# Attention scores from float32r halves, with heads interleaved by on-chip transfers

## The chip, the core and the metric

The kernel runs on one core of a Trainium2 chip. Its engines work side by side, each with its own queue of instructions: TensorE (PE, with weight loads as PEld), VectorE (DVE), ScalarE (ACT), GpSimd (POOL) and SyncE (SP), which here only issues DMAs. The metric is the device time of one execution in microseconds (us); three executions are given by their median and ends.

## The reference, cut to what matters

The program is a block of four sublayers on x of 8 batches x 512 tokens x 256 channels. Only the first, an attention with selected queries, is touched:

```python
q, k, v = split_heads(xn @ Wq + bq), split_heads(xn @ Wk + bk), split_heads(xn @ Wv + bv)
scores   = einsum('bhqd,bhkd->bhqk', q, k) / sqrt(16)          # 16 heads of 16 channels
sparsity = scores.max(-1) - scores.mean(-1)
top      = top_k(sparsity, 307)                                # of 512 queries
out[top] = softmax(scores[top]) @ v                            # the others stay zero
x = x + out @ Wo + bo
```

After it come a routed feed-forward layer, a gated linear attention with a SwiGLU layer, and the feed-forward layer again.

## The kernel before, in words

**What a score is for.** Every score is computed twice. `max_one` (line 531) makes a 128 x 512 tile with queries on the partitions and reduces it to row maxima on DVE (L541). `exp_one` (line 545) makes the transposed tile, keys on the partitions, and ACT takes its exponential (L553). `weigh` (L558) multiplies the exponentials by the values; a column of ones among the values gives the denominators. Keys are centred over the tokens (`xcT`), so that the mean of the scores needs no computing, and exponentials are of score minus maximum.

**Layout.** A chunk `m` is half of the channels, 8 heads, in four strips of 32 partitions. A strip holds an even head (e = 0) in its first 16 rows and an odd one (e = 1) in the last 16. Scores need one head at a time, so each head is kept in a copy in which the other head's rows are zero: `qs[e]` is made with a scale `own` that is one or zero by row, and `ks[e]` with a scale `kept`. One row of the other head's 16 does work: in `ks[e]` it is set to one, and in `qs[e]` it takes the negated row maximum, so that the product over 32 rows gives score minus maximum at once.

**Maxima to queries.** `place_maxima` (line 494) turns the maxima of a batch's chunk by a TensorE transpose (`mxT`, L501), negates them on ACT (L506), and issues transfers of 4 rows x 128 on SP (L510): 8 into `qs` and 8 into `neg`, the tile from which `top_queries` later chooses queries on DVE. These are the placements.

**Steps.** The loop at line 664 goes over steps n, 16 per batch (two chunks, two parities e, four tiles). Step n computes maxima for batch n // 16 and exponentials for the step 16 earlier (LAG), and weighs the exponentials of one step before. A step has two halves; each issues four score products, two for exponentials and two for maxima, one in each row strip. After the first half comes the weighing, after the second one piece of a `front` (line 392): the transposition, projection and evacuation of a later batch, cut in 14 pieces by `yield`. Fronts 0 and 1 run early; the front of batch b >= 2 has its pieces in the steps from LEAD + 16 (b - 2), and none in the two steps of EMPTY, which weigh in two half widths instead. From step 112 on, every fourth step does one more step of maxima. Maxima end at step 123; the exponentials go on to step 143, while DVE makes the choice of queries.

**Evacuation of a front.** Per chunk, q is read from PSUM twice (L449 on DVE; in the early fronts L444 on ACT) and k twice on ACT (L461).

**PSUM.** Score tiles come from two rings of banks, three for exponentials (`bank`) and four (`bank_m`) for maxima, fronts and `mxT`; one bank accumulates the weighing.

**Order.** Each engine takes its instructions in the order of the program. That holds for SP's transfers too: one that waits holds up those behind it.

Of the kernel before, what the change touches and what calls it, by code (L numbers as in the profile page):

```python
# [10 lines left out]
F32 = mybir.dt.float32  # L11
U8 = mybir.dt.uint8
I32 = mybir.dt.int32
# [5 lines left out]
P = 128  # L19
# [20 lines left out]
def block_kernel(ctx: ExitStack, tc: tile.TileContext, t: dict, out: bass.AP):  # L40
# [57 lines left out]

    share = ctx.enter_context(tc.tile_pool(name="share", bufs=1))
# [3 lines left out]
    with ExitStack() as outer:  # L103
# [28 lines left out]
        rden = a_out.tile([P, L], F32, name="rden")  # L132
        work = a_out.tile([P, L + 8], F32, name="work")
        m8 = a_out.tile([P, 8], F32, name="m8")

# [42 lines left out]
        with ExitStack() as inner:  # L178
# [15 lines left out]
            def load_heads(name, src, eng):  # L194

                wp = a2.tile([P, NC2, L], F32, tag="k1", name=name + "_pad", bufs=3)
                eng.dma_start(out=wp, in_=src.rearrange("(c p) m -> p c m", p=P))
                w = a1.tile([P, NC2, D], F32, name=name)
                nc.gpsimd.tensor_copy(
                    w.rearrange("p c (h d) -> p (c h) d", d=DH),  # L200
                    wp.rearrange("p c (h q) -> p (c h) q", q=32)[:, :, 0:DH],
                )
                return w

            def load_head_column(name, src, eng):
                w = a1.tile([P, NC2], F32, name=name)
                for r in range(2):
                    eng.dma_start(
                        out=w[64 * r : 64 * r + 64, :],
                        in_=src.rearrange("(j q) g -> j q g", q=32)[:, 0:DH, r::2],  # L210
                    )
                return w
# [14 lines left out]
            marks = a1.tile([P, 3, 2], F32, name="marks")  # L227
            own, one, kept = (marks[:, i, :] for i in range(3))
            nc.vector.tensor_reduce(own[:, 0:1], head_of, AX.X, ALU.add)
            nc.vector.tensor_scalar(own[:, 1:2], own[:, 0:1], -1.0, 1.0, ALU.mult, ALU.add)  # L230
            for e in range(2):
                nc.vector.tensor_reduce(
                    one[:, e : e + 1], ident[:, DH * (1 - e) :: 32], AX.X, ALU.add
                )
            nc.vector.tensor_scalar(kept, one, -1.0, 1.0, ALU.mult, ALU.add)
            bq_own = a1.tile([P, 2, NC2], F32, name="bq_own")
            for e in range(2):
                nc.vector.tensor_scalar(bq_own[:, e, :], bq, own[:, e : e + 1], None, ALU.mult)

            bk_kept = a1.tile([P, 2, NC2], F32, name="bk_kept")  # L240
            nc.gpsimd.tensor_tensor(bk, bk, bk, ALU.subtract)
            for e in range(2):
                nc.vector.tensor_scalar(
                    bk_kept[:, e, :], bk, kept[:, e : e + 1], one[:, e : e + 1],
                    ALU.mult, ALU.add,
                )
# [4 lines left out]
                a1.tile([P, 4 * H // 2, 2, 32], F32, tag=f"va{i}", name=f"va{i}")  # L251
# [3 lines left out]
            def clear_values(i, late=None):  # L255
                va = vas[i]
                if late is not None:
                    nc.gpsimd.tensor_copy(va[0:1, 0, 0, 0:1], late)
                nc.gpsimd.memset(va, 0.0)
                nc.gpsimd.memset(va[:, :, 0, DH : DH + 1], 1.0)  # L260
                nc.gpsimd.memset(va[:, :, 1, 0:1], 1.0)

            clear_values(0)
            for i in range(2):
                nc.gpsimd.memset(den[i], 1.0)

# [85 lines left out]
            )  # L352
            for _ in batch_stats([0]):
                pass
# [26 lines left out]

            fronts = {}
# [9 lines left out]
            def front(b, pick, alone):  # L392
# [3 lines left out]
                xnT = a2.tile([P, NC2, L], F32, tag="xnT", name=f"xnT{b}")  # L396
# [4 lines left out]
                for c in range(NC2):  # L401
# [17 lines left out]
                qs = [  # L419
                    a2.tile([P, NC2, L], F32, tag=f"q{e}", name=f"q{e}_{b}", bufs=3)  # L420
                    for e in range(2)
                ]
                ks = [
                    a2.tile([P, NC2, L], F32, tag=f"k{e}", name=f"k{e}_{b}", bufs=3)
                    for e in range(2)
                ]
                va = vas[b % 3]
                fronts[b] = (qs, ks, va, xcT)
# [7 lines left out]
                for m in range(NC2):  # L436
                    ps = pick(f"q_ps{b}")
                    for c in range(NC2):
                        project(ps, wq, xnT, m, c)
                        if c == 0:  # L440
                            yield
                    for e in range(2):
                        if alone and (b + m > 0 or e == 0):
                            nc.scalar.activation(  # L444
                                qs[e][:, m, :], ps, AF.Identity,
                                bias=bq_own[:, e, m : m + 1], scale=own[:, e : e + 1],
                            )
                        else:
                            nc.vector.tensor_scalar(  # L449
                                qs[e][:, m, :], ps, bq[:, m : m + 1], own[:, e : e + 1],  # L450
                                ALU.add, ALU.mult,
                            )
                    yield

                    ps = pick(f"k_ps{b}")
                    for c in range(NC2):
                        project(ps, wk, xcT, m, c)
                        if c == 0:
                            yield
                    for e in range(2):  # L460
                        nc.scalar.activation(  # L461
                            ks[e][:, m, :], ps, AF.Identity,
                            bias=bk_kept[:, e, m : m + 1], scale=kept[:, e : e + 1],
                        )
                    yield
                for kp in range(2):
# [11 lines left out]
                    for e in range(2):  # L478
                        home = va[
                            :, 16 * kp : 16 * kp + 16, e, DH * e : DH * e + DH  # L480
# [12 lines left out]

            def place_maxima(b, m, es, tiles=range(4)):
# [10 lines left out]
                negT = a2.tile([32, P], F32, tag="negT", name=f"negT{b}")  # L505
                nc.scalar.mul(negT[0:rows, :], pt[0:rows, 0:P], -1.0)  # L506

                def place(target, r):
                    for i, k in enumerate(tiles):
                        nc.sync.dma_start(  # L510
                            out=target[:, bass.ts(k, P)],
                            in_=negT[r + 4 * i : r + 4 * i + 4, :],
                        )

                def to_queries():
                    for i, e in enumerate(es):
                        place(fronts[b][0][e][DH * (1 - e) :: 32, m, :], n * i)

                def to_choice():
                    for i, e in enumerate(es):  # L520
                        r = row_of(b, m, e)
                        place(neg[r : r + 4, :], n * i)
# [8 lines left out]
            def max_one(b, m, e, k, j, pick):  # L531


                qs, ks = fronts[b][0:2]
# [3 lines left out]
                nc.tensor.matmul(  # L538
                    s, qs[e][rows, m, bass.ts(k, P)], ks[e][rows, m, :], start=True, stop=True
                )  # L540
                nc.vector.tensor_reduce(  # L541
                    mx[:, b % 4, m, e, r : r + 1], s, AX.X, ALU.max
                )

            def exp_one(b, m, e, kt, j, pick):
                qs, ks = fronts[b][0:2]
                rows = bass.ts(j, 32)
                s = pick(f"s2_{b}")
                nc.tensor.matmul(  # L549
                    s, ks[e][rows, m, bass.ts(kt, P)], qs[e][rows, m, :], start=True, stop=True  # L550
                )
                ex = a2.tile([P, L], F32, tag="e", name=f"e{b}", bufs=10)
                nc.scalar.activation(ex, s, AF.Exp, scale=1.0 / DH**0.5)  # L553
                return ex

            def weigh(av, m, e, kt, es, va, queries):
                for j in range(4):
                    nc.tensor.matmul(  # L558
                        av[32 * j : 32 * j + 32, queries],
                        va[:, 8 * kt + 4 * m + j, e, :],  # L560
# [4 lines left out]
            def take(b, m, e, av):  # L565

                st = a2.tile([P, L], F32, tag=f"st{e}", name=f"st{e}_{b}")
# [36 lines left out]
            LEAD = 14  # L604
            EMPTY = (13, 14)
# [22 lines left out]
            def finish(item, part=None):  # L628
# [10 lines left out]
                weigh(av, m, e, kt, es, fronts[b][2], queries)  # L639
# [24 lines left out]
            for n in range(len(steps) + LAG + 1):  # L664
# [4 lines left out]
                empty = batch + 2 >= NB or i in EMPTY  # L669
                halves = LAG < n <= len(steps) and empty and (n - LAG - 1) % 4 > 0  # L670
                if ahead is None:
                    if here is not None:
                        for i in range(4):
                            es[i] = exp_one(*here, i, bank if i % 2 else bank_m)
                    for part in (0, 1) if halves else (None,):
                        finish(behind, part)
                elif here is None:
                    for i in range(4):
                        max_one(*ahead, i, bank if i % 2 else bank_m)
                    place_full(n)  # L680
                else:

                    for half in range(2):
                        for i in range(4):
                            if i % 2 == half:
                                es[i] = exp_one(*here, i, bank)
                            else:
                                max_one(*ahead, i, bank_m)
# [9 lines left out]
                if ahead is not None:  # L698
                    all_maxima(ahead)
                    if n >= 112 and n % 4 == 0 and coming < len(steps):  # L700
                        ahead = steps[coming]
                        for i in range(4):
                            max_one(*ahead, i, bank_m)
                        all_maxima(ahead)

                if n < LEAD:
# [17 lines left out]
                    while done < 22 * (n + 1) // LEAD:  # L724
                        next(pieces, None)
                        done += 1
                else:
                    if n >= LAG:
                        next(later, None)
                    if (n - LEAD) % 16 == 12 and batch + 3 < NB:  # L730
                        norm(batch + 3)
                        add_bias(batch + 3)
                    if (n - LEAD) % 16 == 0:
                        pieces = (
                            front(batch + 2, bank_m, False) if batch + 2 < NB else iter(())
                        )
# [682 lines left out]
```

## Time and profile before

| | us |
|---|---|
| median of 3 executions (lowest, highest) | 1606.35 (1604.23, 1610.29) |
| the profiled execution | 1611.02 |
| its span, first to last instruction | 1609.3 |
| first score product | 15.43 |
| first product for an exponential (step 16) | 61.0 |
| step 112, by its extra maxima | 465 |
| last product for a maximum ends | 515 |
| last exponential ends | 563 |
| L541 on DVE: 512 reductions, mean | 328.1, 0.683 |
| L553 on ACT: 512 exponentials, mean | 276.0, 0.597 |
| L538 on PE: 1024 records of max products, busy | 294.6 |
| L549 on PE: 1024 records of exp products, busy | 291.9 |
| L558 on PE: 1240 records of weighings, busy | 142.6 |

The granted TensorE clock is 0.995 of full speed. A fp32 product shows as two records, each with a weight load. Records of products in different row strips overlap, so a group's busy time is the union of its records, not their sum. The execution's time is 1.7 us over its span.

### The profile page before, as it was taken

What the parts mean: (1) busy time and instruction counts of PE and PEld (TensorE: products, weight loads), DVE (VectorE), ACT (ScalarE), POOL (GpSimd) and SP (SyncE); (2) the same over time, 40 slices, a digit from 0 to 9 for tenths busy, and PEclk for the clock granted to TensorE, in tenths of its full rate; (3) what the DMA queues carried; (4) which work ended last, traced back from release to release, by engine and by line L of the source; (5) the groups of instructions that cost most, each with busy time, mean ns of one, the idle gap of its engine ahead of it and who ended that gap; (6) DMA issues with size and microseconds to landing.
All of it is one profiled execution on the core that took longest, in us unless ns stands there. A gap on an engine that the chain in (4) does not pass through costs nothing.

```text
span 1609.3 us, 19898 instructions
## 1 busy us (share of the span) xinstructions
PE 1575.9 (98%) x7444; PEld 811.8 (50%) x7444; DVE 956.4 (59%) x1982; ACT 682.3 (42%) x1249; POOL 390.2 (24%) x470
## 2 busy tenths in 40 slices
PE   7999999999999999999999999999999999999999
PEld 3333323323233276655564567546545655756666
DVE  7888767677676984538744565456275533354332
ACT  5556656666566833442255125432531442121110
POOL 4423112021000151115433333234253320000000
PEclk9999999999999999999999999999999999999999
DMA  4100000000000051100000001000000010011100
GB/s 122 31 3 2 3 3 3 2 2 3 3 3 3 2 171 28 27 14 13 1 1 0 1 1 27 1 0 1 0 1 1 0 27 0 21 34 40 40 27 26
DMA packets 24968, 27.62 MB, mean 17 GB/s; under 512 B 6888, under 2 KB 21416, under 8 KB 24872
## 3 DMA queue, kind: packets, MB, share of 16 engines
q1 hardware_dynamic: 24056, 25.31, 5.5%
q8 instruction: 58, 0.95, 0.2%
q10 hardware_dynamic: 816, 1.05, 0.2%
q14 instruction: 38, 0.31, 0.1%
HBM read 21.24 MB, written 4.33 MB: 16 GB/s over the span
## 4 chain that ended last, share of the span: by engine, by line
PE 79%; DVE 11%; ACT 4%; POOL 3%; issue 2%; DMA 1%; SPq 0%; POOLq 0%; ACTq 0%; DVEq 0%
PE y_ps L1016 16%; PE h_ps L1042 10%; PE s L538 9%; PE s L549 9%; PE av L558 8%; PE swi_ps L1069 7%; PE proj_ps L1155 7%; DVE pr L1188 2%; DVE pr L1178 2%; PE q_ps L431 2%; POOL o L1205 2%; PE v_ps L470 2%; PE k_ps L431 2%; PE gla_y L1280 2%; DVE w L1180 2%
## 5 line engine op out<-in xcount | busy, mean ns | idle before, releaser
L541 DVE TENSOR_REDUCE mx<-s 128x1 f32<-128x512 f32 x512 | 328.1, 683 | 119.1 <-PE s L549 62.4
L553 ACT ACTIVATE e<-s 128x512 f32<-128x512 f32 x512 | 276.0, 597 | 180.2 <-PE s L549 104.6
L538 PE MATMUL s<-k,q 32*128 32x512 f32 x1024 | 294.6, 639 | 1.4 <-ACT k L461 0.9
L549 PE MATMUL s<-q,k 32*128 32x512 f32 x1024 | 291.9, 639 | 0.0
L1016 PE MATMUL y_ps<-w,h 128*128 128x256 f32 x1024 | 234.8, 384 | 7.4 <-DVE h L1051 6.8
L1042 PE MATMUL h_ps<-xnT,w 128*128 128x512 f32 x512 | 228.1, 594 | 0.0
L1016 PEld LDWEIGHTS y_ps<-w,h 128*128 128x128 f32 x1024 | 193.9, 192 | 45.3 <-issue 10.2
L1042 PEld LDWEIGHTS h_ps<-xnT,w 128*128 128x128 f32 x512 | 94.7, 190 | 106.3 <-issue 104.3
L558 PE MATMUL av<-e,va 128*32 128x512 f32 (+1 forms) x1240 | 142.6, 530 | 1.4 <-ACT st L568 1.4
L1051 DVE TENSOR_TENSOR h<-h,mk 128x512 f32<-128x512 f32 x128 | 95.7, 762 | 79.5 <-ACT h L1050 61.4
L1050 ACT ACTIVATE h<-h_ps,b 128x512 f32<-128x512 f32 x96 | 65.3, 685 | 177.2 <-PE h_ps L1042 177.2
L538 PEld LDWEIGHTS s<-k,q 32*128 32x128 f32 x1024 | 91.4, 183 | 89.6 <-DVE mx L541 50.5
L549 PEld LDWEIGHTS s<-q,k 32*128 32x128 f32 x1024 | 89.6, 183 | 74.7 <-ACT e L553 52.6
L1027 DVE TENSOR_TENSOR xres<-xres,y_ps 128x512 f32<-128x512 f32 x47 | 32.2, 685 | 155.6 <-PE y_ps L1016 118.4
L1069 PE MATMUL swi_ps<-zT,w_up 128*128 128x512 f32 x256 | 122.4, 598 | 0.3 <-DVE h L1078 0.3
L1069 PE MATMUL swi_ps<-zT,w_gate 128*128 128x512 f32 x256 | 122.3, 596 | 0.0
L1016 PE MATMUL y_ps<-w_down,h 128*128 128x256 f32 x512 | 117.7, 380 | 0.8 <-DVE h L1078 0.8
L1155 PE MATMUL proj_ps<-q_w,rT 128*128 128x512 f32 x256 | 115.4, 594 | 1.0 <-DVE gate L1161 0.9
L1016 PEld LDWEIGHTS y_ps<-w_down,h 128*128 128x128 f32 x512 | 95.1, 190 | 19.8 <-issue 7.2
L1075 ACT ACTIVATE h<-swi_ps 128x512 f32<-128x512 f32 x64 | 38.2, 596 | 143.5 <-PE swi_ps L1069 143.4
L1205 POOL TENSOR_TENSOR o<-o,pr 128x512 f32<-128x512 f32 (+2 forms) x56 | 82.2, 1469 | 59.0 <-DVE pr L1188 57.4
L924 POOL TENSOR_TENSOR xres<-xres,b 128x512 f32<-128x512 f32 x32 | 40.0, 1271 | 206.3 <-ACT row L863 183.8
(219 smaller groups left out, 1742.1 us busy)
## 6 DMA issues: line engine op xcount, KB each, us to landing
mk<-md SPq DMA_DIRECT2D x32, 256.0 KB
out<-xres SPq DMA_DIRECT2D x15, 256.0 KB
xres<-in_L_attn_a_x SPq DMA_DIRECT2D x7, 512.0 KB
q<-negT SPq DMA_DIRECT2D x128, 2.0 KB
neg<-negT SPq DMA_DIRECT2D x128, 2.0 KB
w<-in_f_w1T SPq DMA_DIRECT2D x1, 1024.0 KB
w<-in_f_w2T SPq DMA_DIRECT2D x1, 1024.0 KB
w_gate<-in_b_w_gateT SPq DMA_DIRECT2D x1, 1024.0 KB
```

Of the source, the lines that this page charges most:

```text
L538: nc.tensor.matmul(s, qs[e][rows, m, bass.ts(k, P)], ks[e][rows, m, :], start=True, stop=True)
L541: nc.vector.tensor_reduce(mx[:, b % 4, m, e, r : r + 1], s, AX.X, ALU.max)
L549: nc.tensor.matmul(s, ks[e][rows, m, bass.ts(kt, P)], qs[e][rows, m, :], start=True, stop=True)
L553: nc.scalar.activation(ex, s, AF.Exp, scale=1.0 / DH**0.5)
L558: nc.tensor.matmul(av[32 * j : 32 * j + 32, queries], va[:, 8 * kt + 4 * m + j, e, :], es[j][:, queries], start=(kt == 0), stop=(kt == 3 a ...
L1016: nc.tensor.matmul(y[0][:, bass.ts(i, D)], h[f][:, bass.ts(2 * u + i, P)], w[:, f, :], start=(f == 0), stop=(f == NF - 1),)
L1042: nc.tensor.matmul(ps, w1[:, c, bass.ts(f, P)], xT[g][:, c, :], start=(c == 0), stop=(c == NC2 - 1),)
L1050: nc.scalar.activation(hf, ps, AF.Relu, bias=b1[:, f : f + 1])
L1051: nc.vector.tensor_tensor(hf, hf, mk[g][:, f, :], ALU.mult)
L1069: nc.tensor.matmul(ps, w[:, c, bass.ts(f, P)], zT[g][:, c, :], start=(c == 0), stop=(c == NC2 - 1),)
L1155: nc.tensor.matmul(ps, rT[b // G4][:, c, bass.ts(b % G4, P)], q_w[:, c, m], start=(c == 0), stop=(c == NC2 - 1),)
L1205: nc.gpsimd.tensor_tensor(dst, dst, src, ALU.add)
```

## The change: what it does

- **Halves.** q, k and the negated maxima are each split in two tiles of type float32r: `hi`, the rounded value, written by ACT from PSUM, and `lo`, value minus `hi`, written by DVE (`scalar_tensor_tensor`); for the maxima `lo` is written by POOL, in the last batch by DVE.
- **Layout.** The weights' columns are permuted as they are loaded, so that a chunk's rows alternate between an even and an odd head's channels. From `half` tiles, transfers of 64 rows x 512 on SP (`move`) lay out, per chunk, `qh` (q's hi twice, in alternate rows), `ql` (q's lo twice) and `km` (k's hi and lo in alternate rows), each with one plane for each parity e. So all 32 rows of a strip hold one head. Per chunk that is 8 moves for q and 4 for k.
- **Scores.** A maximum's score is two products, `qh` with `km` and `ql` with `km`, summed in PSUM. An exponential's is three: the same two, and one over four rows with `tops`, the halves of the negated maxima of both parities, against `takes`, ones and zeros that choose a parity. `together` issues the four tiles' first products, then their second, then the exponentials' third. With fp32 each score was one product.
- **Placements.** Per chunk 16 transfers into `tops` instead of 8 into `qs`, and 8 into `neg` as before.
- **Values.** One column of ones, between the parities, serves both.
- **Order.** Fronts of batches 2 to 7 begin 7 steps later (LEAD 21 instead of 14) and run values and heads in turn; EMPTY is (14, 15). The early phase keeps its 14 steps (FIRST).
- **Room.** `qh`, `ql`, `km` have four buffers per chunk, `half` four, `tops` three tiles; `xnT` has one buffer, `st` is shared by both parities, `rden` is `neg`.

```diff
             def load_heads(name, src, eng):
-                nc.gpsimd.tensor_copy(
-                    w.rearrange("p c (h d) -> p (c h) d", d=DH),
-                    wp.rearrange("p c (h q) -> p (c h) q", q=32)[:, :, 0:DH],
-                )
+                for e in range(2):
+                    nc.gpsimd.tensor_copy(
+                        w.rearrange("p c (g d e) -> p (c g) d e", d=DH, e=2)[:, :, :, e],
+                        wp.rearrange("p c (g e q) -> p (c g) e q", e=2, q=32)[:, :, e, 0:DH],
+                    )
...
             def load_head_column(name, src, eng):
                 for r in range(2):
-                    eng.dma_start(
-                        out=w[64 * r : 64 * r + 64, :],
-                        in_=src.rearrange("(j q) g -> j q g", q=32)[:, 0:DH, r::2],
-                    )
+                    for e in range(2):
+                        eng.dma_start(
+                            out=w[64 * r + e : 64 * r + 64 : 2, :],
+                            in_=src.rearrange("(j q) g -> j q g", q=32)[e::2, 0:DH, r::2],
+                        )
...
+            def move(dst, src):
+
+                nc.sync.dma_start(out=dst.bitcast(I32), in_=src.bitcast(I32))
+
...
+                def halves(ps, bias):
+
+                    hi, lo = (
+                        a2.tile([P, L], F32, tag="half", name=f"half{b}", bufs=4)
+                        for i in range(2)
+                    )
+                    nc.scalar.activation(hi.bitcast(HALF), ps, AF.Identity, bias=bias)
+                    nc.vector.scalar_tensor_tensor(
+                        lo.bitcast(HALF), ps, bias, hi, ALU.add, ALU.subtract
+                    )
+                    return hi, lo
+
+                def heads_of_chunk(m):
+
+                    qh, ql, km = (
+                        a2.tile([P, 2, L], F32, tag=tag, name=f"{tag}{b}", bufs=4)
+                        for tag in ("qh", "ql", "km")
+                    )
+                    pairs[m] = qh, ql, km
...
-                    for e in range(2):
-                        if alone and (b + m > 0 or e == 0):
-                            nc.scalar.activation(
-                                qs[e][:, m, :], ps, AF.Identity,
-                                bias=bq_own[:, e, m : m + 1], scale=own[:, e : e + 1],
-                            )
-                        else:
-                            nc.vector.tensor_scalar(
-                                qs[e][:, m, :], ps, bq[:, m : m + 1], own[:, e : e + 1],
-                                ALU.add, ALU.mult,
-                            )
+                    for to, half in zip((qh, ql), halves(ps, bq[:, m : m + 1])):
+                        for e in range(2):
+                            for x in range(2):
+                                move(to[x::2, e, :], half[e::2, :])
...
-                    for e in range(2):
-                        nc.scalar.activation(
-                            ks[e][:, m, :], ps, AF.Identity,
-                            bias=bk_kept[:, e, m : m + 1], scale=kept[:, e : e + 1],
-                        )
+                    for x, half in enumerate(halves(ps, bk[:, m : m + 1])):
+                        for e in range(2):
+                            move(km[x::2, e, :], half[e::2, :])
...
                 nc.scalar.mul(negT[0:rows, :], pt[0:rows, 0:P], -1.0)
+                nc.scalar.mul(hi[0:rows, :].bitcast(HALF), pt[0:rows, 0:P], -1.0)
+                eng = nc.vector if b == NB - 1 else nc.gpsimd
+                eng.tensor_tensor(
+                    lo[0:rows, :].bitcast(HALF), negT[0:rows, :], hi[0:rows, :], ALU.subtract
+                )
...
                 def to_queries():
                     for i, e in enumerate(es):
-                        place(fronts[b][0][e][DH * (1 - e) :: 32, m, :], n * i)
+                        for x, half in enumerate((hi, lo)):
+                            place(tops[(2 * b + m) % 3][2 * e + x :: 32, :], half, n * i)
...
             def max_one(b, m, e, k, j, pick):
-                nc.tensor.matmul(
-                    s, qs[e][rows, m, bass.ts(k, P)], ks[e][rows, m, :], start=True, stop=True
-                )
+                def product(i):
+                    nc.tensor.matmul(
+                        s, (qh, ql)[i].bitcast(HALF)[rows, e, bass.ts(k, P)],
+                        km.bitcast(HALF)[rows, e, :], start=(i == 0), stop=(i == 1),
+                    )
...
             def exp_one(b, m, e, kt, j, pick):
-                nc.tensor.matmul(
-                    s, ks[e][rows, m, bass.ts(kt, P)], qs[e][rows, m, :], start=True, stop=True
-                )
+                def product(i):
+                    if i < 2:
+                        keys = km[rows, e, bass.ts(kt, P)]
+                        queries = (qh, ql)[i][rows, e, :]
+                    else:
+                        four = slice(32 * j, 32 * j + 4)
+                        keys = takes[four, e, :]
+                        queries = tops[(2 * b + m) % 3][four, :]
+                    nc.tensor.matmul(
+                        s, keys.bitcast(HALF), queries.bitcast(HALF),
+                        start=(i == 0), stop=(i == 2),
+                    )
...
+            def together(items):
+
+                for i in range(3):
+                    for products, _ in items:
+                        if i < len(products):
+                            products[i]()
+                return [end() for _, end in items]
...
                     for half in range(2):
-                        for i in range(4):
-                            if i % 2 == half:
-                                es[i] = exp_one(*here, i, bank)
-                            else:
-                                max_one(*ahead, i, bank_m)
+                        made = together([
+                            exp_one(*here, i, bank) if i % 2 == half
+                            else max_one(*ahead, i, bank_m)
+                            for i in range(4)
+                        ])
+                        es[half::2] = made[half::2]
...
-            LEAD = 14
-            EMPTY = (13, 14)
+            FIRST = 14
+            LEAD = 21
+            EMPTY = (14, 15)
```

## Prediction

> **What bounds the kernel now.** First the page: which engine is full where.
>
> ```profile
> span 1609.3 us, 19898 instructions
> ...
> PE   7999999999999999999999999999999999999999
> PEld 3333323323233276655564567546545655756666
> DVE  7888767677676984538744565456275533354332
> ACT  5556656666566833442255125432531442121110
> ```
>
> One slice is 40.2 us. The change touches only the attention, slices 1 to 14 (to 564 us); the rest is taken as unchanged. PE stands at 9 throughout, but ends of matmuls are modelled, so I asked the chain of waits from 129 to 465 us:
>
> ```profile
> by line: PE s L538 27.8%; PE s L549 26.7%; PE av L558 24.6%; PE v_ps L470 6.3%; PE q_ps L431 6.3%; PE k_ps L431 6.3%; PE xnT_ps L404 1.6%; PE mxT_ps L501 0.6%
> ```
>
> It is PE alone, over half of it score products. The windows give the other engines' slack in one batch of 16 steps (332 to 399 us; columns: length, then busy time of PE, PEld, DVE, ACT, POOL):
>
> ```profile
> 332.00:399.00 67.00, 67.00 (x450) 20.61 (x444) 47.56 (x78) 41.20 (x79) 10.30 (x9) 1.00 0.01 2
> ```
>
> DVE has 19.4 us free of 67, ACT 25.8. The timeline shows one half step, two exp scores (L549) and two max scores (L538) in four row strips, then its weight loads:
>
> ```profile
> 333.83 0.69 PE L549 MATMUL s<-q,k 32*128 32x512 f32 x1
> 333.84 0.69 PE L538 MATMUL s<-k,q 32*128 32x512 f32 x1
> ...
> 334.37 0.59 PE L549 MATMUL s<-q,k 32*128 32x512 f32 x1
> ...
> 334.90 1.06 PE L558 MATMUL av<-e,va 128*32 128x512 f32 x8
> ```
>
> ```profile
> 333.83 0.18 PEld L549 LDWEIGHTS s<-q,k 32*128 32x128 f32 x1 [0.76 <-ACT e L553]
> ...
> 333.94 0.18 PEld L549 LDWEIGHTS s<-q,k 32*128 32x128 f32 x1
> ```
>
> Each fp32 product is two records. All four strips start within 0.02 us, the second records 0.53 us later, the next work at 334.90: a half costs 1.07 us. Full-width fp32 work prices a record:
>
> ```profile
> 1364.59 13.81 PE y_ps L1016 x64
> ```
>
> That is 0.216 us per 256 columns, so 0.43 for 512, and 1.07 = 0.19 (first load and change of tiling) + 2 x 0.43 + 0.02. A batch needs 32 halves x 1.07 = 34.2, 16 weighings x 1.00 = 16.0, twelve projection pieces x 1.06 and two transposes x 0.59 = 13.9, two mxT x 0.22: 64.6 us. A batch takes 66.5 (placements start at 336.51 and, one batch on, at 402.96), so waiting costs 1.9. PE's sum is the time.
>
> **1. Products in single passes.** A half becomes three rounds over the strips: hi products, lo products, and in the third only the two exps' maxima. No row shows a float32r product. [...] Ends: 0.11 us (a strip takes its second load that much after its first) and 0.86 (the full fp32 product). [...] A half: 0.19 + 3 x 0.215 = 0.84, saving 0.23; because the loads must now be hidden under one pass instead of two I allow 0.02 and take **0.21 per half**: 32 x 0.21 = 6.7 us a batch.
>
> [...] And y_ps repeats each 0.216 us with a 0.19 us load under it. [...]
>
> **2. What joins the other queues in a batch.** DVE: four q operations (L449, 0.80) go, four lo operations (scalar_tensor_tensor; L143 took 0.69) come at about 0.75: equal. ACT: four k operations (0.776) go, four hi at 0.70 (like L413) and two small 0.27 come: equal. POOL: two 32x128 subtractions, about 0.25 each, in an engine 10 of 67 us busy. DVE's sum stays near 47.6 of now some 62 us.
>
> The new wait is lo for hi. It sits in DVE's queue, with the next maxima behind it, and those hold the banks that PE needs. Hi itself queues on ACT behind two exps (1.09). From nothing (ACT ahead) to 1.09 + 0.70 = 1.8 us of idle DVE, four times a batch: 0 to 7.2. DVE's slack of 14 us takes most; today the two q operations (1.53 us in a row) block the queue much alike. I take **1.7 us a batch** reaching PE.
>
> **3. Transfers.** A batch has 24 moves of 64 rows (128 KB) and 48 placements instead of 32, all on SP. SP's rate:
>
> ```profile
> 336.51 4.72 SPq L510 DMA_DIRECT2D q<-negT  x8
> 341.29 5.02 SPq L510 DMA_DIRECT2D neg<-negT  x8
> ```
>
> With gaps 0.59 and 0.63 us each, whether the rows are 512 B (these) or 2 KB (not shown; I take 0.6): 56 x 0.6 + 16 x 0.63 = 44 us of 62. In order, with a step of 3.85 us: a chunk's 24 placements start 9.5 steps into a batch and take 14.6 us, to 13.3; the 8 q moves (issued from 10) follow to 14.6, the 4 k moves (from 12) to 15.2, landed (1.6 us, step 4) at 15.6; they are read from 16. So the cover is 0.4 steps, 1.5 us: I cost them at nothing, but at 0.7 us an issue the 36 would be 2.1 us late, 12 us in six batches, one for one. The second chunk has two steps more. The reused tiles are free: the last exps that read them run in step 31, the moves start in step 32.
>
> **4. The start.** Here nothing hides them.
>
> ```profile
> 12.84 1.73 PE k_ps L431 x4
> 14.60 0.79 ACT k L461
> 15.43 1.18 PE s L538 x8
> ```
>
> q is complete at 12.84: hi by 13.55, lo by 14.3; SP issues four hi and four lo moves by 18.4, four k moves by 20.8. Landing: the last neg transfer left SP at 519.05 and its reader began at 520.21, 1.2 us; with 0.4 for the bulk, 22.4. [...]I take the row: **+7 us**. Four more bias-column loads (0.6 each) delay wk, whose copy ended at 9.2; it is needed near 12.7: hidden.
>
> In the 16 steps of maxima alone (15.4 to 61.1) PE loses 16 x 0.43, but DVE was busy 39.4 of 45.6 and gets six more lo operations, 4.5 us: between 0 and +4.5, I take **+2**.
>
> **5. The rest.** Steps 16 to 111 are six batches: 6 x (6.7 - 1.7) = **-30**. Steps 112 to 123 (465 to 514, an extra maximum step in four): PE loses 3 x 2.1 = 6.4, DVE has 37.2 of 49.2 busy: **-5**. After 514 ACT's exps set the pace (4 x 0.52 us in a row, 9.6 us per four steps) beside DVE's choice (520 to 564); PE's saving is worth nothing, while three more placements stand before the last one to `neg`: **+1.5**, less up to 1 for ACT's 0.3 us waits, so **+0.5**. Later due times move fronts, not their work. Neg doubling as rden, one xnT and shared st are each free more than five steps before reuse: nothing.
>
> Sum: 7 + 2 - 30 - 5 + 0.5 = **-25.5**. The profiled execution, 1611.0 (span 1609.3), becomes 1585.5; the shown median, 1606.35, is 4.7 lower and becomes **1581**. With the ends (start 5 to 9, phase of maxima 0 to 4.5, stalls 0 to 3.5 a batch, late moves 0 to 5, end -2 to 2) the forecast's own range is 1564 to 1600.
>
> **Rivals.**
> (a) DVE takes PE's place: each lo waits its full 1.8 us, 7.2 a batch, more than the 6.7 saved. Then only steps 112 to 123 gain: 1606 + 9.5 - 5 + 3 = 1614; with half of the stall, 3.6, it is 1606 + 9.5 - 5 - 6 x 3.1 = 1592. For it: DVE would stand near 80%. Against: PE now waits only 1.9 a batch with similar blocks.
> (b) Loads not hidden, at each change of round in a strip: one pass is too short for the next load (0.184), because the second buffer frees only as its matmul starts. A further round costs 0.184 + 0.215, a half 0.19 + 0.215 + 2 x 0.40 = 1.20, +0.13 over 216 halves = +28, with start, maxima and end +9.5: 1644. It decides once a further round costs over 0.29 us. For it: two records now give twice the cover. Against: y_ps.
> (c) The products aren't single-pass: two passes each make a half 1.48, +0.41 x 216 = +89 and +9.5: 1704. No row excludes it.
>
> **Chances.** Forecast 0.56, (a) 0.17, (b) 0.17, (c) 0.07, 0.03 left for slower causes unnamed. What a measurement of this kernel tells from no change is about 0.5%, 8 us. Faster takes the forecast and a quarter of (a): 0.60; same most of (a): 0.11; slower the rest: 0.29. The range 1560 to 1646 takes in the forecast, (a) and nearly all of (b); the forecast's own is given above.
>
> **What would show it.** Right: 1024 max and 1536 exp products as one record each, rounds 0.21 to 0.23 us apart, halves near 0.85, placements 61 to 63 us apart per batch instead of 66.5, first maximum near 22 us. (a): DVE idle before lo, waiting for ACT. (b): rounds 0.3 to 0.4 apart. (c): 0.43. Wrong altogether if PE waits on a move's DMA at each batch's first scores, or if the strips of float32r products don't run side by side.

## The result and the profile after

The changed kernel takes **1687.38 us** (median of 4 executions, 1682.39 to 1689.04) where the kernel before takes 1608.32 beside it: 1.049 of the time before, interval 1.0469 to 1.0511. The forecast was 1581, in a range of 1560 to 1646: wrong in sign. The profiled execution is 1689.04, its span 1687.3, 78.0 us longer than before. Medians and ends below are over all executions; ratios leave out two of the version with early key moves, which took over 1.5% longer than its fastest.

The page's head and its rows of 40 slices, now 42.2 us each (the last row is the granted clock, in tenths):

```profile
span 1687.3 us, 21479 instructions
...
PE   6898898999998998999999999999999999999999
PEld 2433343334343335665556556655555566666766
DVE  6876565666565688453874545565445632444342
ACT  3365554555554483434226423622442252221010
...
PEclk9798888899897699999999999999999999999999
```

The attention is slices 1 to 15. PE has 8s there, ACT is mostly at 4 and 5 where it was at 5 and 6, and the clock, 9 in every slice before, goes down to 8, 7 and 6. No row became fuller but that of the weight loads (PEld), which stays at 4 and below. After slice 15 nothing differs: DVE's first normalization after the choice of queries (L143, now L148) starts at 643.0 us instead of 563.9, +79.1 against the span's +78.0.

The chain of waits from 129 to 465 us, by line, was PE alone before. After:

```profile
by line: SPq L384 27.2%; PE s L592 21.2%; PE av L614 15.3%; PE s L566 9.3%; PE v_ps L476 6.8%; ACT e L599 3.9%; issue 3.2%; PE q_ps L428 3.1%; DMA qh<-half 3.0%; PE xnT_ps L408 2.1%; DMA neg<-negT 1.9%; PE k_ps L428 1.6%; ACTq L626 1.4%; PE
```

Over a quarter of it is SP issuing transfers (L384). The milestones below are the transposes `mxT`, one per chunk, so two in a batch; the second ends the first batch's maxima, the 14th comes six batches later, the 18th is the last.

| `mxT` | before | after | difference, forecast and found |
|---|---|---|---|
| second | 67.8 | 78.1 | +9, **+10.3** |
| second to 14th | 401.6 | 460.4 | -30, **+58.7** |
| 14th to last | 47.2 | 55.9 | -5, **+8.7** |
| a batch (4th to 12th, a quarter) | 66.5 | 76.3 | -5.0, **+9.7** |

One batch in windows (from, to, length, then busy time of PE, PEld, DVE, ACT, POOL, and the granted clock):

```profile
189.39:265.20 75.81, 68.43 (x510) 29.34 (x507) 46.39 (x77) 41.37 (x81) 13.65 (x14) 0.89 0.12 44
```

PE is idle for 7.4 us of it, and a mean clock of 0.89, where the trace's clock records hold only the values 1.0 and 0.5, is 22% of the time, 16.7 us, at half rate (17.1 by the records), which loses 8.3 by my estimate. Together 15.7: without them a batch would be about 60, less than before and less than forecast.

**The products themselves went as forecast.** A half step in PE's timeline (start, length), away from the gaps:

```profile
300.30 0.49 PE L592 MATMUL s<-qh,km 32*128 32x512 f32 x1
300.30 0.50 PE L566 MATMUL s<-km,qh 32*128 32x512 f32 x1
...
300.63 0.40 PE L592 MATMUL s<-ql,km 32*128 32x512 f32 x2
...
300.86 0.40 PE L592 MATMUL s<-tops,takes 4*128 4x512 f32 x2
301.18 1.07 PE L614 MATMUL av<-e,va 128*32 128x512 f32 x8
```

Rounds start 0.33 and 0.23 us apart and the half costs 0.88 instead of 1.07. Each product is one record.

**Where the time goes.** PE's timeline at a gap, then ACT's over the same time:

```profile
203.07 0.50 PE L566 MATMUL s<-km,qh 32*128 32x512 f32 x1
207.49 0.79 PE L592 MATMUL s<-qh,km 32*128 32x512 f32 x1 [3.92 <-ACT e L599]
...
209.07 1.93 PE L614 MATMUL av<-e,va 128*32 128x512 f32 x8
```

```profile
201.33 0.59 ACT L624 COPY st<-av 128x512 f32<-128x512 f32 x1
206.29 0.50 ACTq L626 DMA_DIRECT2D den<-st  x1
206.84 1.08 ACT L599 ACTIVATE e<-s 128x512 f32<-128x512 f32 x2 [4.93 <-DMA qh<-half]
```

PE waits for an exponential; the exponentials wait because ACT, which takes its instructions in order, stands 4.4 us before issuing one small transfer, `den<-st` (L626): the denominators of a finished weighing. Its data are ready at 201.9. It is released by the landing of a query move, to which it has no relation in data. After the gap a weighing, 1.07 us in the half step above, takes 1.93: the clock is at half. SP's timeline says why the move is late:

```profile
190.81 8.87 SPq L384 DMA_DIRECT2D tops<-negT  x16
199.72 4.39 SPq L384 DMA_DIRECT2D neg<-negT  x7
204.21 2.43 SPq L384 DMA_DIRECT2D qh<-half  x4
206.75 2.69 SPq L384 DMA_DIRECT2D ql<-half  x4
```

The move is behind 24 placements, at 0.6 us each. The tie between the two transfers is in the trace's semaphores. All 326 transfers that SP and ACT issue between 130 and 465 us share eight (100, 102 to 104 and 106 to 109), in turn in the order of the program, and each waits for the one that it will itself signal. The order of the program here, with the semaphore of both (data waits left out; between the lines shown are three more `qh`, with 102 to 104, and three more `ql`, with 107 to 109):

```
SP   204.21  qh <- half   100
...
SP   206.75  ql <- half   106
...
ACT  206.29  den <- st    100
SP   209.54  km <- half   102
```

ACT's wait for 100 ends at 206.25. ACT's waits between 130 and 465 us (us in total, times, longest) are of two cases, one behind a query move and one behind a placement; in the kernel before, no wait of ACT there was for a DMA:

```profile
ACT e L599 <- PE s L592: 110.7, 124, 2.7
ACT e L599 <- DMA qh<-half: 24.6, 5, 5.3
ACT e L599 <- DMA neg<-negT: 18.3, 4, 4.8
```

That is 4.8 us twice a batch. The kernel before has the same transfer (L570) with the same tie. There SP issued its 16 placements from 336.51 to 346.31 us, and the transfer came up at 349.92; the placement with its semaphore, 108, had been issued at 341.29.

### The profile page after: what moved, and what is told of

It is laid out like the page before. It is cut to its first block, busy times and chain, and to the rows that moved or that the text cites. A ratio compares the mean times of both kernels' runs of the same rounds, so it can differ in the third digit from the quotient of the medians.

```text
span 1687.3 us, 21479 instructions
## 1 busy us (share of the span) xinstructions
PE 1588.1 (94%) x7932; PEld 874.7 (52%) x7932; DVE 954.4 (57%) x1986; ACT 680.6 (40%) x1260; POOL 396.6 (24%) x485
## 4 chain that ended last, share of the span: by engine, by line
PE 63%; DVE 12%; SPq 9%; ACT 5%; issue 4%; POOL 3%; DMA 3%; ACTq 0%; POOLq 0%; DVEq 0%
PE y_ps L1071 15%; PE h_ps L1097 10%; SPq L384 9%; PE swi_ps L1124 7%; PE s L592 6%; PE proj_ps L1210 6%; PE av L614 5%; PE s L566 3%; DVE pr L1243 2%; DVE pr L1233 2%; PE v_ps L476 2%; POOL o L1260 2%; PE gla_y L1335 2%; DVE mx L572 1%; DVE w L1235 1%
## 5 line engine op out<-in xcount | busy, mean ns | idle before, releaser
L572 DVE TENSOR_REDUCE mx<-s 128x1 f32<-128x512 f32 x512 | 324.7, 683 | 144.4 <-PE s L566 140.9
L1071 PEld LDWEIGHTS y_ps<-w,h 128*128 128x128 f32 x1024 | 192.8, 191 | 44.6 <-issue 10.2
L592 PE MATMUL s<-qh,km 32*128 32x512 f32 x512 | 155.1, 545 | 47.2 <-ACT e L599 47.2
L566 PE MATMUL s<-km,qh 32*128 32x512 f32 x512 | 153.0, 550 | 12.0 <-DMA km<-half 8.9
L614 PE MATMUL av<-e,va 128*32 128x512 f32 (+1 forms) x1216 | 162.2, 604 | 2.1 <-ACT st L624 2.0
L592 PEld LDWEIGHTS s<-qh,km 32*128 32x128 f32 x512 | 62.8, 200 | 127.1 <-ACT e L599 90.4
L592 PE MATMUL s<-ql,km 32*128 32x512 f32 x512 | 125.2, 440 | 0.0
L566 PEld LDWEIGHTS s<-km,qh 32*128 32x128 f32 x512 | 61.6, 202 | 121.1 <-DVE mx L572 89.5
L566 PE MATMUL s<-km,ql 32*128 32x512 f32 x512 | 123.4, 450 | 0.0
L592 PE MATMUL s<-tops,takes 4*128 4x512 f32 x512 | 121.4, 431 | 0.0
```

The lines of the kernel that those rows point to most:

```text
L566: nc.tensor.matmul(s, (qh, ql)[i].bitcast(HALF)[rows, e, bass.ts(k, P)], km.bitcast(HALF)[rows, e, :], start=(i == 0), stop=(i == 1),)
L572: nc.vector.tensor_reduce(mx[:, b % 4, m, e, r : r + 1], s, AX.X, ALU.max)
L592: nc.tensor.matmul(s, keys.bitcast(HALF), queries.bitcast(HALF), start=(i == 0), stop=(i == 2),)
L614: nc.tensor.matmul(av[32 * j : 32 * j + 32, queries], va[:, 8 * kt + 4 * m + j, DH * e : DH * e + 2 * DH], es[j][:, queries], start=(kt == ...
L1071: nc.tensor.matmul(y[0][:, bass.ts(i, D)], h[f][:, bass.ts(2 * u + i, P)], w[:, f, :], start=(f == 0), stop=(f == NF - 1),)
```

## The experiments

Theory A: the loss is this held transfer, with the half clock that follows the gap. Rival B: the moves come late for the products that read them. Rival C: float32r products, or PE's new rhythm, lower the clock by themselves. A 2 x 2 came first: each kernel with the transfer on ACT and on GpSimd's queue, so that ACT has no part in it.

**The changed kernel, the transfer on GpSimd.**

```diff
-                nc.scalar.dma_start(out=den[b // 6][r : r + 4, :], in_=st[DH * (1 - e) :: 32, :])
+                nc.gpsimd.dma_start(out=den[b // 6][r : r + 4, :], in_=st[DH * (1 - e) :: 32, :])
```

> The kernel after, with the 32 den transfers issued by GpSimd instead of ACT. Theory A (ACT is held at its den transfer until a transfer far back in SP's queue has landed; exponentials, banks and PE then wait, and the idle PE's clock is halved for a while): no waits of ACT above 2 us at the exponentials, granted clock of the attention back at 0.98 or more, 1575 to 1600 us. Rival B (the moves themselves land late, the scores wait for qh, ql, km): nearly unchanged, 1660 us or more, PE still waiting. Rival C (float32r products bring the clock down whatever waits): stalls gone but clock near 0.87 in the attention, 1630 to 1670 us.

Measured: 1598.76 us (1590.39 to 1612.80), 0.9948 of the time before (0.9931 to 0.9965). A batch takes 60.5 us. The windows from 130 to 394 us, of the changed kernel and of this version:

```profile
130.00:394.00 264.00, 240.47 (x1775) 101.76 (x1775) 165.90 (x283) 144.81 (x280) 46.47 (x56) 0.88 0.13 47
```

```profile
130.00:394.00 264.00, 263.99 (x2223) 113.82 (x2217) 205.00 (x346) 180.26 (x350) 69.92 (x86) 1.00 0.15 56
```

PE is full and the clock whole. One line takes back 89 us. B and C fall: moves, products and rhythm are all still there.

**The same edit in the kernel before** (L570).

> Control: the kernel before with the same edit. All theories: no change, 1600 to 1616 us, clock 0.99; SP's queue is short enough there that ACT's den transfer is not held.

1614.72 us (1611.35 to 1618.06), ratio 1.0039 (1.0024 to 1.0055): dearer by 6 us, not the same. The profiled execution is the fastest of the six; the spans of the others reach 1616.3 us as their granted clock falls from 0.994 to 0.990, where the executions of the kernel before beside it have 0.994 to 0.998. So the 6 us go with a lower clock. Why it is lower stays open.

**The kernel before, with more transfers on SP.** Nothing reads what they write; the products stay fp32. Per chunk 8 more placements into a tile of their own, and in the fronts from batch 2 on 12 transfers of 64 rows x 80; `xnT` gets one buffer to make room.

```diff
+            spare, room = (a1.tile([P, L], F32, name=f"spare{i}") for i in range(2))
+            def more(src, ids):
+                for i in ids:
+                    own = slice(80 * (i // 2), 80 * (i // 2) + 80)
+                    nc.sync.dma_start(out=room[i % 2 :: 2, own], in_=src[i % 2 :: 2, own])
...
+                    if not alone:
+                        more(qs[1][:, m, :], range(8))
...
+                    if not alone:
+                        more(ks[1][:, m, :], range(8, 12))
...
+                def to_spare():
+                    for i, e in enumerate(es):
+                        place(spare[64 * i : 64 * i + 4, :], n * i)
...
+                    to_spare()
```

> The kernel before, fp32 scores as they are, with transfers added on SP that nobody reads: 8 placements per chunk and 12 moves of 64 rows at the q and k evacuations of the fronts of batches 2 to 7 (and one xnT buffer, for room). SP's queue is then as long as after the change. Theory A: about one stall of 4 to 5 us per batch at a den transfer of ACT, clock below 0.97 in the attention, 1630 to 1670 us. Rival B: no change, 1605 to 1615, since no score reads them. Rival C: no change, clock 0.99.

1662.26 us (1661.83 to 1662.47), ratio 1.0331 (1.0314 to 1.0348); a batch 75.6 us. The loss appears without a single float32r product: the clock is 0.95 from 130 to 394 us, PE has a gap of 4.5 to 5.1 us in each batch, and ACT's waits between 130 and 465 us have the same mark:

```profile
ACT e L569 <- DMA spare<-q: 26.0, 4, 6.8
```

**That kernel with the transfer on GpSimd** (the edit of the first experiment).

> e3 with the den transfers issued by GpSimd. Theory A: the stalls go, 1603 to 1618 us, clock 0.99. Rivals B and C: as e3 under them, 1605 to 1615. If e3 is slow and this one too, the added transfers hurt in another way than through ACT (SBUF or ring contention).

1615.55 us (1611.58 to 1615.94), ratio 1.0031 (1.0017 to 1.0045): 47 of the 54 us are gone while every added transfer is still there, and what is left is about what the second experiment showed. The added transfers on SP cost nothing by themselves; the held instruction does.

**The transfer on ACT, but later.** Next, whether it can stay on its queue. Of each chunk's two denominator transfers, the first falls into SP's backlog; it is issued three steps later, behind the last exponential of that step.

```diff
-                    nc.scalar.activation(ex, s, AF.Exp, scale=1.0 / DH**0.5)
+                    exps[:] = [nc.scalar.activation(ex, s, AF.Exp, scale=1.0 / DH**0.5)]
...
-                nc.scalar.dma_start(out=den[b // 6][r : r + 4, :], in_=st[DH * (1 - e) :: 32, :])
+                def send():
+                    nc.scalar.dma_start(
+                        out=den[b // 6][r : r + 4, :], in_=st[DH * (1 - e) :: 32, :]
+                    )
+                if e == 0 and b < NB - 1:
+                    sends.append((n + 3, send))
+                else:
+                    send()
...
+                while sends and sends[0][0] <= n:
+                    with tc.issue_after(exps[-1].ins):
+                        sends.pop(0)[1]()
```

> The changed kernel; the first of each chunk's two denominator transfers (the one that is due in the middle of SP's backlog) stays on ScalarE's queue but is issued 11 us (three steps) later, when SP has caught up. If the loss is the held denominator transfer and nothing of the queue it sits on, the stalls go as they did with the transfer on GpSimd (exponentials never held for over 2 us by anything but the products, a batch in about 60.5 us, clock 1.00 between 130 and 394 us), and without the 6.4 us that the GpSimd queue cost the kernel before: 1592 us, between 1586 and 1598. If the gain of the GpSimd version came from taking work off ScalarE's queue, not from the wait, it stays near 1680.

1598.03 us (1594.07 to 1603.33), ratio 0.9937 (0.9919 to 0.9955), at the upper edge of what was expected; a batch 60.9. One batch in windows, and ACT's waits between 130 and 465 us:

```profile
230.27:291.16 60.89, 60.87 (x510) 26.31 (x507) 46.35 (x77) 41.35 (x81) 13.68 (x14) 1.00 0.15 56
```

```profile
ACT e L599 <- PE s L592: 105.7, 154, 2.2
ACT negT L527 <- issue: 2.5, 11, 0.3
```

PE is busy for 60.87 of 60.89 us at the full clock, with SP as loaded as in the changed kernel. The transfer is on ACT's queue as there; only the wait is gone. The 6 us that this was to save over the GpSimd version (1598.76) did not come.

**One step later instead of three** (`n + 1`).

> The same with the transfer only one step (3.8 us) later: it is then still held, but for about 1.5 us in place of 5.3 where it waits for the first query move, and not at all where it waits for a placement. If the half clock comes only from a gap on TensorE of some 4 us, a hold of 1.5 us is swallowed by the products queued ahead and the clock stays whole: within 0.4% of the version that is three steps late. If every us of hold is paid, and the clock sinks in proportion, it lies 10 to 15 us above that version.

1611.51 us (1602.24 to 1623.80), ratio 1.0015 (1.0001 to 1.0030); a batch 63.5. ACT's waits again:

```profile
ACT e L599 <- DMA ql<-half: 14.8, 6, 2.7
ACT xnT L411 <- DMA neg<-negT: 5.6, 4, 1.6
```

The holds, now of 2.7 us at most, come to 3.9 us a batch (20.4 us in the 5.3 batches of this stretch), and a batch is 2.6 us longer than with three steps. PE's gaps in this stretch are 0.5 to 1.2 us long. After the two longest, of 1.17 and 1.11 us, the clock is at half for some 3.4 us; PE's timeline and the window at the first:

```profile
261.63 0.49 PE L592 MATMUL s<-qh,km 32*128 32x512 f32 x1 [1.17 <-ACT e L599]
...
262.51 1.95 PE L476 MATMUL v_ps<-wv,xnT 128*128 128x256 f32 x4
```

```profile
262.70:266.10 3.40, 3.40 (x18) 1.83 (x21) 1.96 (x5) 0.82 (x3) 0.00 (x0) 0.50 0.30 113
```

Over the stretch the clock is 0.99. So neither expectation held whole: short holds are largely paid, not swallowed, but the clock is lost for little of the time.

**The transfer on SP itself** (`nc.sync`).

> The changed kernel with the denominator transfers on SP itself, in its order, so that ScalarE never waits for SP; what can wait is SP, behind a copy that isn't done, and the copy's buffer. Theory of the held transfer: 1592 us, as three steps late on ScalarE, plus 4 x 0.6 us more of SP a batch, which has cover: 1588 to 1602. If SP's load itself is the bound (44 us of 61 a batch, then 47), the moves come later and the time rises above 1605.

1600.74 us (1593.30 to 1616.07), ratio 0.9953 (0.9934 to 0.9972), within the expected range; a batch 60.5. SP's load is not the bound.

**The three steps' delay in the kernel before.**

> Control: the kernel before with the same three steps' delay. Its SP queue is done by the time the transfer is issued, so nothing is held there and the time is that of the kernel before, 1608 us within 0.3%. A gain of 0.5% or more would say that the wait cost the kernel before something too.

1609.08 us (1603.42 to 1612.88), ratio 0.9997 (0.9985 to 1.0009): there the wait cost nothing.

**The last key moves ahead of the placements.** All three repaired versions stay some 17 to 20 us above the forecast. In the version three steps late the batches were even better than forecast, but the stretch from the 14th `mxT` to the last took 56.4 us, 9.2 more than before. PE's timeline there, then windows of it:

```profile
467.02 0.79 PE L566 MATMUL s<-km,qh 32*128 32x512 f32 x2 [3.50 <-DMA km<-half]
```

```profile
470.00:475.00 5.00, 5.00 (x37) 1.78 (x33) 2.58 (x4) 2.17 (x4) 0.00 (x0) 0.50 0.01 3
...
485.00:490.00 5.00, 5.00 (x30) 2.06 (x30) 3.06 (x6) 1.09 (x2) 2.04 (x2) 0.50 0.02 5
490.00:495.00 5.00, 4.55 (x49) 2.06 (x44) 4.08 (x8) 3.58 (x9) 0.00 (x0) 1.00 0.02 5
```

Here a move is late for the products after all, once: the last batch's keys, at the end of SP's placements, where the extra maxima want them two steps sooner than in other batches. A wait of 3.5 us is followed by 23 us at half the clock. The edit, on top of the three steps' delay:

```diff
-                    yield from values(1)
-                    yield from heads_of_chunk(1)
+                    if b == NB - 1:
+                        yield from heads_of_chunk(1)
+                        yield from values(1)
+                    else:
+                        yield from values(1)
+                        yield from heads_of_chunk(1)
...
-                    nc.scalar.dma_start(
+                    eng = nc.sync if (b, m) == (NB - 3, 1) else nc.scalar
+                    eng.dma_start(
```

> The version three steps late, and in the last front the heads of the second chunk made before the last values, so that their key moves enter SP's queue ahead of 24 placements and not behind them (with the two denominator transfers that this would hold given to SP). In the version three steps late the products waited 3.5 us for these moves (464 to 467 us) and TensorE's records stayed at the half clock until about 490. If a transfer behind the placements is again what costs, the clock in 460 to 540 us comes back from 0.83 to 0.93 or more, the last maximum comes some 10 us sooner (502.5 to about 492), and the time is 1588 us, 1581 to 1595. If the tail is bound by the search for the top queries on VectorE anyway (39 us after the last placement), or the last placements are late by themselves, less than 3 us comes back: 1595 to 1600.

**1589.59 us** (1582.83 to 1608.57), ratio **0.990** (0.9877 to 0.9923). The stretch takes 47.4 us instead of 56.4, the clock in 460 to 540 us is 0.96. The last `mxT` comes at 500.0 all the same, not near 492: this execution had lost some 8 us to the one before it by the 14th, with half the clock from about 73 to 100 us. The version beats both kernels, 98 us below the changed one.

**A clearing on GpSimd three steps later.** In that version PE waited 4.1 us at 40 to 44 us for the second front, which waited for a small operation on GpSimd behind a memset.

```diff
-                    if n in (2, 5):
-                        clear_values(n // 2, maximum_of(n))
+                    if n in (2, 8):
+                        clear_values(1 if n == 2 else 2, maximum_of(n))
```

> The version with early key moves, and GpSimd's second clearing of a value tile three steps later, so that it no longer stands before the small statistics operation that the second batch's front waits for (TensorE was idle for 4.1 us at 40 to 44 us, and at the half clock after it to 50). If a gap of this length is what takes the clock away, the gap falls to some 2 us, the clock of 40 to 50 us comes back from 0.66 to 0.9 or more, and the time is 1585 us, 1578 to 1592. If the half-clock stretch of 70 to 100 us, which that profile shows without a gap of over 0.6 us ahead of it, has a cause of its own (TensorE thinly loaded while VectorE's maxima set the pace, 50 to 70 us), that stretch stays, and the time lies within 0.3% of 1589.6.

1593.36 us (1589.25 to 1594.87), ratio 0.9912 (0.9897 to 0.9928): no different from the version before it. The gap fell to 1.2 us and the clock of 40 to 50 us came back to 1.00; but the windows that follow hold another stretch at half clock (the third number from the end), as the version before it has from 70 to 100 us:

```profile
50.00:60.00 10.00, 9.34 (x45) 4.38 (x46) 10.00 (x19) 2.75 (x9) 5.94 (x23) 1.00 0.42 139
60.00:70.00 10.00, 9.25 (x52) 5.80 (x52) 10.00 (x18) 2.38 (x6) 2.78 (x4) 0.83 0.06 11
70.00:80.00 10.00, 9.74 (x57) 4.16 (x54) 6.09 (x16) 4.36 (x10) 6.97 (x4) 0.50 0.65 217
80.00:90.00 10.00, 10.00 (x76) 3.92 (x72) 6.47 (x14) 4.34 (x8) 3.22 (x16) 0.50 0.02 5
```

DVE is full from 50 to 70 us and PE waits for it in pieces, none over 0.6 us. That this thin load takes the clock away is argued from these rows, not shown: no run filled PE there.

## Why the prediction was wrong

**Part 1, halves: right.** 0.88 us against 0.84 to 0.86. No run shows the 0.215 us that the sum gives a round: the second starts 0.33 after the first, the third 0.23 after the second, the next work 0.32 after the third. Strips load side by side, as in the kernel before (eight loads from 333.83 to 333.96): a half's first four loads start within 0.01 us of each other and the next four 0.1 later. Each takes 0.18 us. The third round's start with the second round's products, at 300.63:

```profile
300.40 0.18 PEld L592 LDWEIGHTS s<-ql,km 32*128 32x128 f32 x1
...
300.63 0.19 PEld L592 LDWEIGHTS s<-tops,takes 4*128 4x128 f32 x2
```

That is as rival (b) had it, but the load, of 0.19 us, is over within the round: the third products follow at 300.86, 0.23 us after the second, not 0.40. The first step of 0.33 is in (b)'s range of signs; fp32 has the same 0.10 over its 0.43 there (0.53). Rivals (b) and (c) are out: a half would have cost 1.20 or 1.48.

**Part 2, lo behind hi: right in kind, too dear.** DVE waits 15.2 us for hi between 130 and 465 us in the version three steps late, 2.7 a batch, inside the bounds of 0 to 7.2; but the 1.7 that I let reach PE don't. There PE waited for DVE for 1.1 us in 335. So a batch is 60.9 us where 61.5 was forecast: the change is worth 5.6 us a batch when nothing is held. Rival (a) is out.

**Part 3, transfers: the step that failed.** "I cost them at nothing", with a cover of 1.5 us. I asked when the moved data would be read. That part held: except for the last batch's keys, no product waited between 130 and 465 us for a move. I did not ask who else waits for SP's queue. The profile showed SP's 16 placements in 10 us and the denominator transfer on ACT; with 24 placements and 12 moves, 44 us of SP a batch as I had worked out, any ACT instruction tied to a place in SP's order was going to meet the backlog. I followed the queue's data and left out its semaphores. The price: 15.4 us a batch (76.3 against 60.9), about half of it the held exponentials (7.4 us of idle PE), the rest half clock. Over six batches that is the 58.7 + 34.1 us between the changed kernel and the repaired one.

**Part 4, the start: right.** First score product at 21.37 instead of 15.43, +5.9 for 7. No run shows the 0.4 us for the bulk in that sum: the last key move had left SP at 20.43, and the product that waits for it started 0.9 later, not 1.6. First product for an exponential at 70.0 instead of 61.0, +9 for 9.

**Part 5, the rest.** Six batches: -30 forecast, -34.1 once nothing is held. The stretch after step 112: -5 forecast, +8.7 in the changed kernel, +9.2 with the transfer late, +0.2 with the key moves early as well. So the 5 us are not there even without a stall; why not wasn't tried. The end: from the last `mxT` to the end of the attention 48.7 us in the changed kernel instead of 47.2, +1.4 for 0.5.

**The sum** of the version with early key moves by these terms: +9.2 start, -26.0 batches, +0.2, +1.3 end, together -15.3; its profiled execution is 1596.1, 15.0 under before's 1611.0 (its median is 1589.6). To the forecast's -25.5 it lacks 5 us in the stretch after step 112 and 4 in the batches, which lost 8 (-26.0 for -34.1) with the half clock of 70 to 100 us. No term of the forecast had the clock in it: I took the 0.995 of before as given. (The ends named for the forecast's own range add up to 1603, not 1600.)

## What to carry to other kernels

When transfers are added to a queue, list every instruction on other engines that waits for a place in that queue, not only the readers of the data: here one small transfer on ACT, whose instructions go in order, held the exponentials behind it for up to 5.3 us. Then look for gaps on TensorE: those of 3.5 to 4.3 us here cost about twice their length (15.4 us a batch for 7.4 us of idle PE), because half the clock followed. The repair was cheap for the 87 to 89 us that it took back in three versions: move the waiting instruction to where the queue has caught up, or to a queue of its own, and put urgent transfers ahead of bulk ones.

## What the runs showed of the hardware

Each of the nine gaps of 3.5 to 4.3 us on PE between 130 and 465 us in the changed kernel, and the one of 3.5 us in the repaired one, was followed by half the clock. So were the two gaps of 1.17 and 1.11 us in the version with one step's delay, while its gaps up to 0.9 us, and one of 1.20 us in the last version, were not. After the nine, half rate set in 1.8 to 4.4 us from the start of the gap. The length of a gap alone does not decide: the two short ones are against it, and so is the stretch at half clock from about 70 us, with no gap over 0.6 us ahead of it.

The way back is longer than the gaps. In the clock records of the traces half rate lasts 6.8 to 13.7 us after the nine gaps (10.2 after the one at 207.49), and 23.9 in the repaired kernel, through windows in which PE was busy for 5.00 of 5.00 us. All these lengths, and the 3.4 us after the two short gaps, are one to seven times 3.4 us; what sets how many stays open.

The repaired versions also scatter more than the kernel before (1582.83 to 1608.57 against 1603.23 to 1610.34 beside it), and their times go with the clock: 0.987 at 1582.83, 0.968 at 1608.57.
